# Transposed score blocks, a leaky step on GpSimd and an earlier mask in a two-layer graph attention kernel

## The chip, the core and the metric

The kernel runs as one program on one core of a Trainium2 chip. The metric is the device time of one execution in microseconds; the profile gives the span from the first to the last instruction of one execution.

## The reference, cut to what matters

There are 16 graphs of 1024 nodes with 256 features, and an adjacency matrix of 0 and 1 (drawn with a share of about 3% ones, and ones on the diagonal).

```python
# layer 0: masked attention with 8 heads of 32, residual
h = relu(layernorm(x))
Q, K, V = h @ Wq.T + bq, h @ Wk.T + bk, h @ Wv.T + bv          # per head
attn = softmax(where(adj == 0, -inf, Q @ K.T * 32 ** -0.5))
x = x + (attn @ V) @ Wo.T + bo
# layer 1: edge scores of one kind where adj == 1, residual
h = relu(layernorm(x))
e_0 = leaky_relu(einsum('bid,bjd->bij', h * a_0[:, 0], h), 0.2)  # e_1..e_3 the same with a_1..a_3
scores = where(adj == 1, e_0, -9e15)                              # then 2: e_1, 3: e_2, 4: e_3
x = x + softmax(scores) @ h
```

The product inside the leaky function is symmetric in i and j: the score of (i, j) is the sum over d of h[i, d] a[d] h[j, d]. The leaky function takes y to y where y is positive and to 0.2 y where it is not.

## The kernel before, in words

The nodes of a graph are cut into 8 tiles of 128 rows, so there are 128 tiles. The main loop has 129 steps `s`, and in each step it works on several tiles at once, at different stages: `now` is the tile whose 8 heads of layer 0 are attended to in this step, `nxt` and `nxt2` are the next two, `was` is the tile before (its output product, its residual `x1`, its norm for layer 1), `gone` the one before that (its normed rows are transposed into `h1T`), `edge` is the tile of layer 1, nine tiles behind `now`, whose scores and softmax are made, `edge_was` the one before (its product with the rows of `h1`, and its output), and `piece` a tile of a later graph whose queries, keys and values are projected.

Each step loops over `h` from 0 to 7, one head of `now` in each turn, and parts of the other tiles' work are put by hand between the heads (`if h == 2: ...`). The kernel stands under a manual schedule: every engine runs its instructions in the order in which the code issues them, and waits at the one whose inputs or buffers aren't ready. The DMA issues of SyncE and GpSimd stand in the same orders.

For each head of `now`, TensorE makes 128 x 1024 scores into one of two PSUM places (`sides[0]`, and `sides[1]` for heads 3, 5 and 7; L435), VectorE adds the mask, writes the result to one of four buffers `p` and keeps the row's extreme (`softmax_max`, L447), ScalarE takes the exponential (L455). Heads 0, 1, 4 and 5 are then transposed by VectorE in blocks (L376) and placed by DMA, the other four by TensorE (L555) with copies by ScalarE (L556). Then come the products with the values (L490).

For the edge tile, `prepare` makes `ha`, the tile's columns of `h1T` times `a_0` (GpSimd, L577, at h = 4 of the step before); `score` multiplies it with all of `h1T` into `sides[1]`, one half of 512 columns at h = 0 and one at h = 1 (L587); `softmax_max` at h = 2 adds the mask, changes the sign and keeps the row's smallest value `top` (VectorE, L601), from which a small instruction makes the leaky value `nmx` (L606); `leak` at h = 4 applies the leaky step to the 128 x 1024 values in place (VectorE, L609); `softmax_exp` at h = 6 takes the exponential (ScalarE, L613). Since the sign is changed, the leaky step is a minimum: min(0.2 y, y).

The mask of a tile: the adjacency rows are loaded into `adj` (one buffer) at h = 4, two tiles ahead. At h = 3 of the step before its use, `flag` on ScalarE writes into `neg` and sums up which kinds of edges occur (L427), and then `mask` on GpSimd writes the mask over it (L415). A tile's mask is kept until its turn as edge tile.

The norm of `was` and of the next `piece` (`norms`, at h = 5) takes sums on VectorE (L188, L189) and then a chain of small GpSimd instructions (L162 to L178). `was.normed` (ScalarE, L523) uses it at h = 7, `gone.turn_normed` (TensorE, L530) and `turned_normed` (ScalarE, L534) follow in the next step at h = 0 and 1. `reciprocals` at h = 1 makes `wide` on GpSimd (L474) from the sums of the heads, `turned_reciprocals` at h = 2 copies its transposed form `recT` (ScalarE, L484), `add_bias` at h = 2 adds `bo` to the loaded rows `xb` (GpSimd, L419), and `edge_was.load_nodes` at h = 2 issues a load on GpSimd's queue (L619).

The last graph's edge tiles 1 to 7 come after the loop, in a tail where `sides` alternate and nothing of layer 0 runs. `layer_1_of_kinds` is a second way for layer 1, taken only for graphs with other kinds of edges than 0 and 1.

Of the kernel before, what the change touches and what calls it, by code (L numbers as in the profile page):

```python
# [8 lines left out]
F32 = mybir.dt.float32  # L9
# [5 lines left out]
ALU = mybir.AluOpType  # L15
AX = mybir.AxisListType

P = 128
HEADS = 8
HD = 32  # L20
# [3 lines left out]
SLOPE = 0.2  # L24
# [18 lines left out]
def gnn_kernel(  # L43
# [18 lines left out]
    nc = tc.nc  # L62
    B, N, D = x.shape
    NT = N // P
# [319 lines left out]
        return pT.rearrange("p (a j q) -> p j a q", a=NB, j=NT)  # L384


    h1s, h1Ts, x1ds, masks = {}, {}, {}, {}
    kinds_seen = const.tile([P, B * NT], F32, name="kinds_seen")

    class Attend:  # L390
# [122 lines left out]
        def keep(self):  # L513
            if self.t == 0:
                x1ds[self.b] = dram.tile([N, D], F32, tag=f"x1d{self.b}", name=f"x1d_{self.b}", bufs=1)
            nc.sync.dma_start(out=x1ds[self.b][self.rows, :], in_=self.x1)

        def normed(self):
            if self.t == 0:
                h1s[self.b] = graph.tile([P, NT, D], F32, tag="h1", name=f"h1_{self.b}")  # L520
                h1Ts[self.b] = graph.tile([P, NC, N], F32, tag="h1T", name=f"h1T_{self.b}")
            r, shift = self.norm
            nc.scalar.activation(  # L523
                h1s[self.b][:, self.t, :], self.x1, AF.Relu, bias=shift[:, 0:1], scale=r[:, 0:1]
            )
# [6 lines left out]

        def turned_normed(self):
            nc.scalar.copy(  # L534
                h1Ts[self.b][:, :, self.rows].rearrange("p c (b k) -> p c b k", b=NB),
                self.h1_ps.rearrange("p c (k b) -> p c b k", b=NB),
            )

# [20 lines left out]
    class Edges:  # L559


        def __init__(self, b, t, last=False):
            self.b, self.t = b, t
            self.rows = slice(t * P, (t + 1) * P)
            self.side = sides[t % 2 if last else 1]
            self.tags = {"sel": ("p", 4), "pT1": ("pT", 7)} if last else {}
            if last and t % 2:
                self.tags |= {"ha": ("hT", 1), "x1b": ("x1", 1)}
# [5 lines left out]
        def prepare(self):  # L574
            self.ha = self.buffer("ha", [P, NC, P])
            for c in range(NC):
                nc.gpsimd.tensor_scalar(  # L577
                    self.ha[:, c].rearrange("p (k b) -> p k b", b=NB),
                    h1Ts[self.b][:, c, self.rows].rearrange("p (b k) -> p k b", b=NB),
                    a_t[:, c, 0:1], 0.0, ALU.mult, ALU.add,  # L580
                )

        def score(self, nh):
            cols = slice(nh * HALF, (nh + 1) * HALF)
            self.e = self.side
            for c in range(NC):
                nc.tensor.matmul(  # L587
                    self.e[:, cols],
                    lhsT=self.ha[:, c, :],
                    rhs=h1Ts[self.b][:, c, cols],  # L590
                    start=(c == 0),
                    stop=(c == NC - 1),
                )

        def softmax_max(self):
            self.sel = self.buffer("sel", [P, N])
            top = small.tile([P, 1], F32, tag="top")  # L600
            nc.vector.tensor_tensor_reduce(  # L601
                out=self.sel, in0=self.e, in1=masks[self.b, self.t], scale=-1.0, scalar=3e38,
                op0=ALU.add, op1=ALU.min, accum_out=top,
            )
            self.nmx = small.tile([P, 1], F32, tag="nmx1")
            nc.vector.scalar_tensor_tensor(self.nmx, top, SLOPE, top, ALU.mult, ALU.min)  # L606

        def leak(self):
            nc.vector.scalar_tensor_tensor(self.sel, self.sel, SLOPE, self.sel, ALU.mult, ALU.min)  # L609

        def softmax_exp(self):
            self.total = small.tile([P, 1], F32, tag="total")
# [30 lines left out]

    def layer_1_of_kinds(b):
        h1 = graph.tile([P, NT, D], F32, tag="h1", name=f"h1g_{b}")
        h1T = graph.tile([P, NC, N], F32, tag="h1T", name=f"h1Tg_{b}")
        for t in range(NT):
            rows = slice(t * P, (t + 1) * P)
            xt = work.tile([P, D], F32, tag="x1", bufs=1)
            nc.sync.dma_start(out=xt, in_=in_order(x1ds[b][rows, :]))  # L650
            mv = stats_place(1)
            stats_of(xt, mv[:, 0, :])
            r, shift = norm_of(mv)
            nc.scalar.activation(h1[:, t, :], xt, AF.Relu, bias=shift[:, 0:1], scale=r[:, 0:1])
            tr = by_chunk((early, brief)[t % 2])
            for c in range(NC):
                nc.tensor.transpose(tr[:, c, :], h1[:, t, c * P : (c + 1) * P], ident)
            nc.scalar.copy(h1T[:, :, rows], tr)
        for t in range(NT):
            rows = slice(t * P, (t + 1) * P)  # L660
            at = work.tile([P, N], I32, tag="adj", bufs=1)
            nc.sync.dma_start(out=at, in_=adj[b, rows, :])
            xt = work.tile([P, D], F32, tag="x1b", bufs=1)
            nc.sync.dma_start(out=xt, in_=in_order(x1ds[b][rows, :]))

            code = work.tile([P, N], BF16, tag="neg", bufs=KEPT)
            nc.gpsimd.tensor_scalar(code, at, 5.0, 0.0, ALU.min, ALU.max)
            sel = work.tile([P, N], F32, tag="sel", bufs=1)
            nc.vector.memset(sel, NEG_INF)
            for k in range(N_KINDS):  # L670
# [15 lines left out]
                nc.vector.copy_predicated(sel, is_k, e)  # L686
            nc.vector.scalar_tensor_tensor(sel, sel, SLOPE, sel, ALU.mult, ALU.max)
            nmx = small.tile([P, 1], F32, tag="nmx1")
            nc.vector.tensor_reduce(nmx, sel, AX.X, ALU.max, negate=True)
            total = small.tile([P, 1], F32, tag="total")  # L690
            nc.scalar.activation(sel, sel, AF.Exp, bias=nmx, scale=1.0, accum_out=total)
            pT = ptp.tile([P, NT, P], F32, tag="pT1", name="pT1g", bufs=1)
            for half in range(2):
                turn_half(sel, pT, half)
            o = late
            for j in range(NT):
                nc.tensor.matmul(o, lhsT=pT[:, j, :], rhs=h1[:, j, :], start=(j == 0), stop=(j == NT - 1))
            rec = small.tile([P, 1], F32, tag="rec1")
            nc.vector.reciprocal(rec, total)
            ot = work.tile([P, D], F32, tag="ot", bufs=1)  # L700
            nc.vector.scalar_tensor_tensor(ot, o, rec, xt, ALU.mult, ALU.add)
            nc.sync.dma_start(out=out[b, rows, :], in_=ot)
# [18 lines left out]
    with tc.manual_schedule():  # L721
# [48 lines left out]
        for s in range(B * NT + 1):  # L770
# [9 lines left out]
            for h in range(HEADS):  # L780
# [25 lines left out]
                    now.softmax_max(h)  # L806
                if h == 6 and edge_was:
                    edge_was.store()
                if h == 4 and edge:
                    edge.leak()  # L810


                if ending:
# [1 line left out]

                if h == 1 and gone:
                    gone.turned_normed()


                if h == 3:  # L820
# [27 lines left out]
                if h == 1:  # L848
# [6 lines left out]
                    if piece_was:  # L855
                        piece_was.write_again()
                if h == 2:
                    if piece_was:
                        piece_was.values()
                    if was:  # L860
                        was.turn_reciprocals()
                        was.turned_reciprocals()
                        was.add_bias()
                    if edge_was:
                        edge_was.load_nodes()
                if h == 3:
                    if nxt:
                        nxt.load_queries()
                        nxt.flag()
                        nxt.mask()  # L870
                if h == 4:
                    if was:
                        was.output()
# [44 lines left out]
        for i in range(1, len(tiles) + 2):  # L918
# [9 lines left out]
            if i >= 2:  # L928
                tiles[i - 2].load_nodes()
            if edge:  # L930
                edge.softmax_max()
                edge.leak()
                edge.softmax_exp()
# [58 lines left out]
```

## Time and profile before

| | |
|---|---|
| Time, three runs | 3210.05, 3190.67, 3208.38 us; median 3208.38 us |
| Span of the profiled execution | 3197.8 us, 97634 instructions, mean granted TensorE clock 0.985 |
| TensorE busy, matmuls (PE) | 3033.3 us, 95% |
| VectorE busy (DVE) | 2797.9 us, 87% |
| ScalarE busy (ACT) | 2454.3 us, 77% |
| GpSimd busy (POOL) | 1728.1 us, 54% |
| DMA | 762.90 MB, mean 239 GB/s |

The profiled execution's own time is its span: the profile page gives no other. A row of the timeline reads: start in us, length in us, engine, line of the kernel, operation, output and input, shapes, count, and in brackets how long the engine had been idle before it and what released it. In a group, "x120 | 146.0, 1216" means 120 instructions, 146.0 us in all, 1216 ns each. A busy share is an average over stages and engines work beside each other; what a piece of work costs depends on who waits for it.

### The profile page before, as it was taken

What the parts mean: (1) busy time and instruction counts of PE and PEld (TensorE: products, weight loads), DVE (VectorE), ACT (ScalarE), POOL (GpSimd) and SP (SyncE); (2) the same over time, 40 slices, a digit from 0 to 9 for tenths busy, and PEclk for the clock granted to TensorE, in tenths of its full rate; (3) what the DMA queues carried; (4) which work ended last, traced back from release to release, by engine and by line L of the source; (5) the groups of instructions that cost most, each with busy time, mean ns of one, the idle gap of its engine ahead of it and who ended that gap; (6) DMA issues with size and microseconds to landing.
All of it is one profiled execution on the core that took longest, in us unless ns stands there. A gap on an engine that the chain in (4) does not pass through costs nothing. (4 is left out here: it accounts for less than half of the span.)

```text
span 3197.8 us, 97634 instructions
## 1 busy us (share of the span) xinstructions
PE 3033.3 (95%) x36018; PEld 2216.3 (69%) x36018; DVE 2797.9 (87%) x5111; ACT 2454.3 (77%) x4829; POOL 1728.1 (54%) x3883
## 2 busy tenths in 40 slices
PE   5889999999999999999999999999999999998998
PEld 3667767777677777777677777777767677776663
DVE  3888989899898998989899998998989889898984
ACT  3887878788787877878788787887878778787761
POOL 2555555555555555555555655555555655555541
PEclk8999999999999999999999999999999999999999
DMA  6787788887888788788887878788887878888653
GB/s 226 219 244 233 227 273 233 259 240 231 270 240 272 226 253 249 226 277 234 252 238 230 275 233 273 230 254 263 235 272 226 269 228 232 267 240 249 194 161 91
DMA packets 747156, 762.90 MB, mean 239 GB/s; under 512 B 71281, under 2 KB 692209, under 8 KB 746673
## 3 DMA queue, kind: packets, MB, share of 16 engines
q1 hardware_dynamic: 678432, 542.34, 58.3%
q0 software_dynamic: 65040, 210.03, 20.3%
q8 instruction: 290, 4.75, 0.6%
q10 hardware_dynamic: 3200, 4.19, 0.4%
q14 instruction: 194, 1.58, 0.1%
HBM read 252.98 MB, written 167.77 MB: 132 GB/s over the span
## 5 line engine op out<-in xcount | busy, mean ns | idle before, releaser
L455 ACT ACTIVATE p<-p,nmx 128x1024 f32<-128x1024 f32 x1024 | 1178.5, 1151 | 249.6 <-DVE nmx L447 248.9
L447 DVE CUSTOM_DVE_ANT_0 p<-s,neg 128x1024 f32<-128x1024 f32 x1024 | 1233.3, 1205 | 92.0 <-issue 49.8
L435 PE MATMUL s<-k,qt 128*128 128x512 f32 x2048 | 795.0, 469 | 77.6 <-DMA qt<-qd 57.4
L415 POOL TENSOR_SCALAR neg<-adj 128x1024 bf16<-128x1024 int32 x128 | 466.8, 3647 | 411.8 <-ACT neg L427 411.8
L376 DVE STREAM_TRANSPOSE blocks<-p 128x1024 f32<-128x1024 f32 x520 | 642.3, 1235 | 11.3 <-ACT p L613 10.8
L556 ACT COPY pT<-trp 128x512 f32<-128x512 f32 x1024 | 543.6, 581 | 86.5 <-PE trp L555 78.6
L490 PE MATMUL acc<-pT,v 128*32 128x128 f32 x16384 | 525.1, 277 | 25.7 <-DMA pT<-blocks 24.3
L555 PE MATMUL trp<-ident,p 128*128 128x128 f32 x4096 | 534.7, 274 | 0.1
L555 PEld LDWEIGHTS trp<-ident,p 128*128 128x128 f32 x4096 | 480.9, 141 | 72.5 <-ACT pT L556 3.0
L490 PEld LDWEIGHTS acc<-pT,v 128*32 128x32 f32 x16384 | 450.7, 111 | 97.6 <-DVE ot L640 41.2
L631 PE MATMUL acc<-h,pT 128*32 128x256 f32 x8192 | 495.8, 383 | 4.0 <-DVE ot L640 3.2
L435 PEld LDWEIGHTS s<-k,qt 128*128 128x128 f32 x2048 | 330.3, 192 | 210.2 <-issue 122.6
L587 PE MATMUL s<-h1T,ha 128*128 128x512 f32 x992 | 471.1, 598 | 0.0
L631 PEld LDWEIGHTS acc<-h,pT 128*32 128x32 f32 x8192 | 242.6, 110 | 208.4 <-issue 58.7
L474 POOL COPY wide<-rec 128x256 f32<-128x256 f32 x128 | 50.8, 397 | 491.4 <-DVE rec L472 491.4
L321 POOL DMA_DIRECT2D kd<-halves x240 | 168.8, 703 | 228.7 <-DVE halves L294 216.2
L601 DVE CUSTOM_DVE_ANT_0 sel<-s,neg 128x1024 f32<-128x1024 f32 x120 | 147.0, 1225 | 126.4 <-PE s L587 126.4
L587 PEld LDWEIGHTS s<-h1T,ha 128*128 128x128 f32 x992 | 171.5, 193 | 124.1 <-issue 124.1
L455 ACT ACTIVATION_READ_ACCUMULATOR p<-p,nmx 128x1 f32 x1024 | 193.4, 189 | 0.0
L484 ACT COPY recT<-acc 128x256 f32<-128x256 f32 x128 | 47.8, 373 | 177.3 <-PE acc L480 177.3
L273 PEld LDWEIGHTS acc<-hT,wkT 128*128 128x128 f32 x960 | 120.8, 197 | 76.7 <-issue 47.3
L273 PE MATMUL acc<-hT,wkT 128*128 128x128 f32 x960 | 144.3, 295 | 27.3 <-DVE halves L294 26.1
(126 smaller groups left out, 4025.1 us busy)
## 6 DMA issues: line engine op xcount, KB each, us to landing
pT<-blocks SPq DMA_DIRECT2D x2560, 128.0 KB, 3.1
qt<-qd SPq DMA_DIRECT2D x128, 512.0 KB, 5.9
adj<-in_adj POOLq DMA_DIRECT2D x127, 512.0 KB, 5.5
qd<-halves SPq DMA_DIRECT2D x240, 256.0 KB, 4.6
k<-kd POOLq DMA_DIRECT2D x120, 512.0 KB, 6.8
kd<-halves POOLq DMA_DIRECT2D x240, 128.0 KB, 3.4
kd<-halves SPq DMA_DIRECT2D x240, 128.0 KB, 3.2
xb<-in_x POOLq DMA_DIRECT2D x128, 128.0 KB, 3.4
```

What stands on the lines that cost most here:

```text
L273: nc.tensor.matmul(ps, lhsT=wT[:, fc, oc * P : (oc + 1) * P], rhs=(self.hT, self.hTm)[which][:, fc, :], start=(fc == 0), stop=(fc == NC - 1),)
L321: queue.dma_start(out=kds[self.b][oc, :, :, twice, self.cols], in_=halves.rearrange("p (w n) -> p w n", w=2),)
L376: nc.vector.transpose(blocks.rearrange("p b j q -> p j b q"), p)
L415: nc.gpsimd.tensor_scalar(self.neg, self.adj, 0.0, MASKED, ALU.is_equal, ALU.mult)
L435: nc.tensor.matmul(self.ps[:, cols], lhsT=self.qt[:, h, :], rhs=keysets[self.b][h][:, cols], start=True, stop=True,)
L447: nc.vector.tensor_tensor_reduce(out=p, in0=sides[h in (3, 5, 7)], in1=self.neg, scale=-SCALE, scalar=FLOOR, op0=ALU.add, op1=ALU.min, acc ...
L455: nc.scalar.activation(p, p, AF.Exp, bias=nmx, scale=-1.0, accum_out=self.sums[:, h : h + 1])
L490: nc.tensor.matmul(sums_place[r * HD : (r + 1) * HD, g * P : (g + 1) * P], lhsT=vs[self.b][:, j, place_of(h) : place_of(h) + HD], rhs=self ...
L555: nc.tensor.transpose(tr[:, j, :], p[:, jj * P : (jj + 1) * P], ident)
L556: copy(pT[:, half * 4 : half * 4 + 4, :], tr)
L587: nc.tensor.matmul(self.e[:, cols], lhsT=self.ha[:, c, :], rhs=h1Ts[self.b][:, c, cols], start=(c == 0), stop=(c == NC - 1),)
L631: nc.tensor.matmul(sums_place[a * HD : (a + 1) * HD, :], lhsT=self.pT[:, j, a], rhs=h1s[self.b][:, j, :], start=(j == 0), stop=(j == NT - 1),)
```

## The change

There are three parts.

The scores of layer 1 are symmetric before the leaky step. With the change, an edge tile t multiplies only for the column blocks t to 7. After that, ScalarE copies the blocks right of the diagonal from PSUM into a new place `mirror` (`keep`, at h = 1 and h = 2, one instruction for each contiguous place), and later tiles get their blocks left of the diagonal by a transpose of the kept copy on TensorE. `h1T` becomes one buffer for all graphs, and `mirror` has 16 blocks of 128 x 128, which are used again as they are read.

The leaky step of the edge tiles in the main loop goes from VectorE to GpSimd, and is issued at the end of h = 3 and not at h = 4. `softmax_max` scales by -0.2, and the leaky value is y + 4 min(y, 0): on GpSimd two instructions for the row's extreme and two for each quarter of 256 columns. The last graph's tiles in the tail keep it on VectorE.

`flag` and `mask` move from h = 3 to h = 2, where they stand ahead of `values`, the reciprocals' transposes, `add_bias` and `edge_was.load_nodes`.

```diff
+    h1T = const.tile([P, NC, N], F32, name="h1T")
+    mirror = const.tile([P, NT // 2, NT // 2, P], F32, name="mirror")
+    def mirrored(t, first, end):
+        half = NT // 2
+        if t >= half:
+            return [mirror[:, first - t - 1 : end - t - 1, t - half, :]]
+        places = []
+        for j in range(first, min(end, half)):
+            row, at = (half - 1, t) if j == half - 1 else (half - 2, t + j - 1)
+            places.append(mirror[:, row, at : at + 1, :])
+        if end > half:
+            places.append(mirror[:, t, max(first, half) - half : end - half, :])
+        return places
+    def mirrored_block(t, j):
+        return mirrored(t, j, j + 1)[0][:, 0, :]
...
         def score(self, nh):
-            cols = slice(nh * HALF, (nh + 1) * HALF)
-            self.e = self.side
-            for c in range(NC):
-                nc.tensor.matmul(
-                    self.e[:, cols],
...
+            first, end = nh * NT // 2, (nh + 1) * NT // 2
+            for j in range(first, min(end, self.t)):
+                block = self.side[:, j * P : (j + 1) * P]
+                nc.tensor.transpose(
+                    block.rearrange("p (b k) -> p k b", b=NB), mirrored_block(j, self.t), ident
+                )
+            cols = slice(max(first, self.t) * P, end * P)
+            if self.t < end:
+                for c in range(NC):
+                    nc.tensor.matmul(
+                        self.side[:, cols],
+                        lhsT=self.ha[:, c, :],
+                        rhs=h1T[:, c, cols],
...
+        def keep(self, nh):
+            first, end = max(nh * NT // 2, self.t + 1), (nh + 1) * NT // 2
+            for place in mirrored(self.t, first, end) if first < end else ():
+                width = place.shape[1]
+                blocks = self.side[:, first * P : (first + width) * P]
+                nc.scalar.copy(
+                    place.rearrange("p j (k b) -> p j k b", b=NB),
+                    blocks.rearrange("p (j b k) -> p j k b", b=NB, k=HD),
+                )
+                first += width
...
-                out=self.sel, in0=self.e, in1=masks[self.b, self.t], scale=-1.0, scalar=3e38,
-                op0=ALU.add, op1=ALU.min, accum_out=top,
+                out=self.sel, in0=self.side, in1=masks[self.b, self.t], scale=-SLOPE, scalar=3e38,
+                op0=ALU.add, op1=ALU.min, accum_out=self.top,
...
-            nc.vector.scalar_tensor_tensor(self.nmx, top, SLOPE, top, ALU.mult, ALU.min)
-        def leak(self):
-            nc.vector.scalar_tensor_tensor(self.sel, self.sel, SLOPE, self.sel, ALU.mult, ALU.min)
+        def leak(self):
+            if self.last:
+                self.nmx = small.tile([P, 1], F32, tag="nmx1")
+                for to, y in ((self.nmx, self.top), (self.sel, self.sel)):
+                    nc.vector.scalar_tensor_tensor(to, y, 1 / SLOPE, y, ALU.mult, ALU.min)
+                return
+            g = nc.gpsimd
+            less = small.tile([P, 1], F32, tag="less1")
+            g.tensor_scalar(less, self.top, 0.0, 1 / SLOPE - 1, ALU.min, ALU.mult)
+            g.tensor_tensor(self.nmx, self.top, less, ALU.add)
+            part = N // 4
+            for i in range(4):
+                sel = self.sel[:, i * part : (i + 1) * part]
+                less = work.tile([P, part], F32, tag="less", bufs=1)
+                g.tensor_scalar(less, sel, 0.0, 1 / SLOPE - 1, ALU.min, ALU.mult)
+                g.tensor_tensor(sel, sel, less, ALU.add)
...
-                if h == 4 and edge:
-                    edge.leak()
...
+                if h in (1, 2) and edge:
+                    edge.keep(h - 1)
...
                 if h == 2:
+                    if nxt:
+                        nxt.flag()
+                        nxt.mask()
                     if piece_was:
                         piece_was.values()
...
                 if h == 3:
                     if nxt:
                         nxt.load_queries()
-                        nxt.flag()
-                        nxt.mask()
+                    if edge:
+                        edge.leak()
...
             if edge:
+                edge.keep(0)
+                edge.keep(1)
                 edge.softmax_max()
```

More of the change, by code (lines that the diff above doesn't have):

```diff
@@ L384, in placed @@
         return pT.rearrange("p (a j q) -> p j a q", a=NB, j=NT)
-    h1s, h1Ts, x1ds, masks = {}, {}, {}, {}
+    h1s, x1ds, masks = {}, {}, {}
+    h1T = const.tile([P, NC, N], F32, name="h1T")
[13 more added lines that the diff above has]
+        return mirrored(t, j, j + 1)[0][:, 0, :]
     kinds_seen = const.tile([P, B * NT], F32, name="kinds_seen")
@@ L520, in normed @@
                 h1s[self.b] = graph.tile([P, NT, D], F32, tag="h1", name=f"h1_{self.b}")
-                h1Ts[self.b] = graph.tile([P, NC, N], F32, tag="h1T", name=f"h1T_{self.b}")
             r, shift = self.norm
@@ L534, in turned_normed @@
             nc.scalar.copy(
-                h1Ts[self.b][:, :, self.rows].rearrange("p c (b k) -> p c b k", b=NB),
+                h1T[:, :, self.rows].rearrange("p c (b k) -> p c b k", b=NB),
                 self.h1_ps.rearrange("p c (k b) -> p c b k", b=NB),
@@ L562, in __init__ @@
         def __init__(self, b, t, last=False):
-            self.b, self.t = b, t
+            self.b, self.t, self.last = b, t, last
             self.rows = slice(t * P, (t + 1) * P)
@@ L578, in prepare @@
                     self.ha[:, c].rearrange("p (k b) -> p k b", b=NB),
-                    h1Ts[self.b][:, c, self.rows].rearrange("p (b k) -> p k b", b=NB),
+                    h1T[:, c, self.rows].rearrange("p (b k) -> p k b", b=NB),
                     a_t[:, c, 0:1], 0.0, ALU.mult, ALU.add,
@@ L583, in score @@
         def score(self, nh):
-            cols = slice(nh * HALF, (nh + 1) * HALF)
-            self.e = self.side
-            for c in range(NC):
-                nc.tensor.matmul(
-                    self.e[:, cols],
[L589 to L592, printed above, removed]
-                )
+            first, end = nh * NT // 2, (nh + 1) * NT // 2
[3 more added lines that the diff above has]
+                    block.rearrange("p (b k) -> p k b", b=NB), mirrored_block(j, self.t), ident
+                )
@@ new lines, in score @@
+            cols = slice(max(first, self.t) * P, end * P)
[5 more added lines that the diff above has]
+                        rhs=h1T[:, c, cols],
+                        start=(c == 0),
+                        stop=(c == NC - 1),
+                    )
[9 more added lines that the diff above has]
+                first += width
@@ L598, in softmax_max @@
         def softmax_max(self):
             self.sel = self.buffer("sel", [P, N])
-            top = small.tile([P, 1], F32, tag="top")
+            self.top = small.tile([P, 1], F32, tag="top")
             nc.vector.tensor_tensor_reduce(
-                out=self.sel, in0=self.e, in1=masks[self.b, self.t], scale=-1.0, scalar=3e38,
-                op0=ALU.add, op1=ALU.min, accum_out=top,
-            )
-            self.nmx = small.tile([P, 1], F32, tag="nmx1")
-            nc.vector.scalar_tensor_tensor(self.nmx, top, SLOPE, top, ALU.mult, ALU.min)
@@ L645, in layer_1_of_kinds @@
         h1 = graph.tile([P, NT, D], F32, tag="h1", name=f"h1g_{b}")
-        h1T = graph.tile([P, NC, N], F32, tag="h1T", name=f"h1Tg_{b}")
         for t in range(NT):
```

## The prediction

> **What bounds the kernel now.** I read the table by stretches first, then one ordinary step of the main loop engine by engine, then the list of waits. Four consecutive steps, cut from mask to mask:
>
> ```profile
> 1282.30:1305.50 23.20, 23.20 (x284) 17.15 (x283) 21.73 (x42) 19.22 (x39) 12.98 (x30) 1.00 0.80 227
> 1305.50:1328.69 23.19, 23.19 (x284) 17.13 (x283) 21.73 (x42) 19.24 (x39) 12.99 (x30) 1.00 0.80 240
> ```
>
> The columns are length, then busy time of PE, weight load, DVE, ACT and GpSimd (POOL). PE is busy for the whole 23.20 us at full granted clock: PE sets the ordinary step. DVE (21.73) and ACT (19.22) follow, POOL has 12.98. From the first edge tile's maximum (267.61) to that of step 127 (3084.58) lie 118 steps in 2816.97 us, so the mean step is 23.87 us: 23.2 and a few longer ones around the key loads.
>
> A busy share hides order, so the second view is POOL's own order in that step, and where ACT stands beside it:
>
> ```profile
> 1282.30 3.65 POOL L415 TENSOR_SCALAR neg<-adj 128x1024 bf16<-128x1024 int32 x1 [3.24 <-ACT neg L427]
> 1286.05 0.98 POOL L577 TENSOR_SCALAR ha<-h1T,a_t 128x128 f32<-128x128 f32 x2
> 1286.96 0.60 POOL L406 DMA_DIRECT2D adj<-in_adj  x1
> 1287.74 0.22 POOL L162 TENSOR_SCALAR ve<-mv 128x2 f32<-128x2 f32 x1 [0.18 <-DVE mv L189]
> ...
> 1292.54 0.23 POOL L178 TENSOR_SCALAR shift<-shift 128x2 f32<-128x2 f32 x1
> ...
> 1300.89 0.88 POOL L419 TENSOR_TENSOR xb<-xb,bo_t 128x256 f32<-128x256 f32 x1
> 1301.56 0.70 POOL L619 DMA_DIRECT2D x1b<-x1d  x1
> 1305.50 3.64 POOL L415 TENSOR_SCALAR neg<-adj 128x1024 bf16<-128x1024 int32 x1 [3.24 <-ACT neg L427]
> ```
>
> ```profile
> 1289.99 1.13 ACT L613 ACTIVATE sel<-sel,nmx 128x1024 f32<-128x1024 f32 x1
> ...
> 1292.81 0.60 ACT L523 ACTIVATE h<-x,shift,r 128x256 f32<-128x256 f32 x1
> ...
> 1304.17 1.13 ACT L427 ACTIVATE neg<-adj,less_half 128x1024 bf16<-128x1024 int32 x1
> ```
>
> This is a loop through two in-order queues. ACT's check of kinds (L427) releases POOL's mask (L415); behind it stand the two ha products, the adjacency load and the norm's chain, which ends at 1292.77; ACT's normed tile (L523) starts 0.04 us later; ACT then works through its exponentials to the next L427. The loop's POOL half is 10.5 us, its ACT half 12.7 us. It closes in one step only because ACT has idle places in it:
>
> ```profile
> POOL neg L415 <- ACT neg L427: 411.8, 128, 27.8
> ACT recT L484 <- PE acc L480: 177.3, 128, 1.5
> ACT h L523 <- POOL shift L178: 32.8, 32, 5.0
> ```
>
> (us in total, times, longest.) ACT waits for PE and DVE, and already 32 times for POOL's norm. POOL's 46% of idle time is therefore not all free: most lies in the half where it waits for ACT.
>
> **The change, part by part.** All prices are against the profiled execution, span 3197.8 us. The three runs of before gave 3190.67 to 3210.05, median 3208.38, so span and median differ by 0.3% and I add nothing between them. About 1% is what a measurement of this kernel can tell from no change.
>
> *PE, score blocks.* Before, two halves of 4 matmuls took 1.88 us each, 0.47 us per block of 128 columns. Now tile t transposes t blocks and multiplies 8 - t. Transposes in the trace go 8 in 1.03 us, 0.13 us each. With 3.5 blocks per tile on average: 3.5 x (0.47 - 0.13) = 1.2 us less PE per step.
>
> *DVE.* The leaky step (L609, 1.22 us) and its small one (L606, 0.37 us) go: 1.6 us of 21.7.
>
> *ACT, copies kept.* 13 copies per 8 tiles. From L556 (512 columns, 581 ns) and L534 (256 columns, 371 ns) the price is 0.16 us plus 0.82 ns per column: 0.58, 0.48, 0.37 and 0.27 us for 4, 3, 2 and 1 blocks. The second call averages 0.43 us per step, the first 0.20: 0.63 us. Their slots are on ACT's half of the loop. They also guard sides[1], which scores(3) overwrites; but the tile's maximum (DVE, ends at 1301.4) does that later than the copy would (about 1300.6), so that guard is hidden.
>
> *Check and mask one step earlier.* On ACT the check moves ahead of recT (0.37 us) and of one exponential (1.15 us). On POOL the mask now stands ahead of xb+bo and the x1b load, which were done in its waiting time before: they come behind it and cost 0.68 + 0.58 us by their spacing. xb+bo is needed by the residual on DVE, some 6 us later even in a step of 23.2 us, the x1b load by the store later still, at h = 6: hidden.
>
> *POOL, the leaky step.* Ten instructions: two on one column, 0.23 and 0.20 us; four pairs on 256 columns; each waits for the one before, and waiting neighbours in the norm's chain stand 0.08 us apart. The second of a pair is a two-input add of the shape of L419: 0.86 us (0.72 at its quickest in the last steps). The first, minimum and multiply with one f32 input, is not in the trace. Bounds: the copy L474 of 256 columns, 0.40 us; the mask, (3.65 - 0.22) / 1022 = 3.35 ns per column, hence 1.07 us. Nearest is ha (L577), f32 to f32 with two operations: 0.50 us for 128 columns against 0.22 for 2, 2.25 ns per column, hence 0.79 us. I take 0.79. Sum: 0.59 + 4 x (0.79 + 0.86 + 0.16) = 7.8 us, from 5.7 (0.40 and 0.72) to 9.0 us.
>
> The Trainium skill (GPSIMD Engine Reference, sections 3.1 and 4.1) prices one-input work near line rate, about 1.03 cycles a column at 1.2 GHz, and two-input adds at 2.6 cycles, and advises the vector engine for elementwise work. Of the rows the copy agrees (0.83 ns per column), ha and the mask do not (2.25 and 3.35). By the page the leaky step would be an estimated 6.0 us and the total some 3515 us; slower too.
>
> *The loop, closed again.* Behind the leaky step stand, on POOL, ha (0.91 us by spacing), the adjacency load (0.68) and the norm's chain (5.03); ACT's edge exponential waits for the leaky step, ACT's normed tile for the norm, and behind these wait the exponentials and so PE's transposes. POOL's half: 3.72 mask + 1.26 + 7.84 + 0.91 + 0.68 + 5.03 = 19.4 us, plus 5 key loads of 0.6 us per 8 steps, 0.4. ACT's half, back to back: 0.07 latency, 0.60 normed, three exponentials at 1.15, two pairs of copies at 1.06, 0.37 h1T, 0.63 kept copies, 1.23 check, 0.08 latency = 8.55 us. Together 28.4 us. The same sum without the leaky step is 20.5 us, below PE's 23.2: the leaky step alone turns the slack into the bound. PE's and DVE's savings then buy nothing, since both wait.
>
> Against the mean step: 28.4 - 23.87 = 4.5 us. 119 steps hold an edge tile and a full set of heads: +535 us. In the tail the leaky step stays on DVE and PE sets the pace (7.2 us per tile); at most 28 transposes x 0.34 = 9 us are saved there, while the loop's last step, short of other work, loses about 5. I book -3. 3197.8 + 535 - 3 = 3730 us.
>
> **The rivals.**
>
> *Hidden on POOL (the other side).* POOL's busy share says 11 us are free in each step; then PE's 1.2 us count: 3197.8 - 119 x 1.2 = 3055 us. It decides if the whole leaky step takes less than 23.87 - 20.5 = 3.4 us, that is 0.7 us for a pair with its gaps. Against it: the add alone took 0.72 us at its quickest, and ACT waits for POOL already.
>
> *Cheap first operation.* At the copy's rate and the quickest add, the leaky step is 5.7 us, the loop 26.2 us: 3197.8 + 119 x 2.3 = 3475 us. For it: one f32 input. Against: ha, the same form, is slower than the copy.
>
> *Dear first operation.* At the mask's rate the loop is 29.5 us, and PE may enter it:
>
> ```profile
> 3118.86 6.19 PE L587 MATMUL s<-h1T,ha 128*128 128x512 f32 x8
> 3124.88 3.60 PE L587 MATMUL s<-h1T,hT 128*128 128x512 f32 x8
> ```
>
> After PE had idled 3.3 us the same eight matmuls took 6.19 us, then 3.60. Two waits of nearly 4 us in each step could slow PE's transposes in ACT's half by some 0.5 us. 119 x 6.1 more: about 3925 us.
>
> TensorE: Matmul & The Clock Gate in the Trainium skill (part 1) puts half rate after an idle window of about 3.4 us, in line with these two rows. By it PE would run slow after each stall, an estimate of under 2 us per step, which PE, with 6 us free, can mostly pay.
>
> **How the numbers follow.** Forecast 0.65, cheap first operation 0.16, dear 0.15, hidden 0.04. The predicted time is the forecast's, 3730 us. The range runs between the two prices of the unknown operation, 3470 to 3930 us. Faster by over 1% comes only from the hidden case, 0.03; within 1%, 0.01 for a part of it eaten by the copies; slower, 0.96.
>
> **What the changed profile would show.** Right: steps of 28 us; ACT's edge exponential waiting some 3.6 us a step for POOL's last leaky add (POOL gets there 12.9 us after the check, ACT after 9.3), ACT's normed tile 3.8 us a step for POOL's norm, both over 400 us in total; the wait of the mask for the check still there; PE's busy time down by about 145 us and its share near 78%; POOL near 70%. The pairs near 1.65 us. Wrong: PE above 90% busy with POOL's waits unchanged (hidden case), or a wait that ends last elsewhere, on DVE or on the copies kept.

## The result, and the profile after

| | before | after |
|---|---|---|
| Time, median of 4 runs | 3209.22 us | 3945.12 us (3940.7 to 3954.88) |
| Ratio after to before | | 1.231, 95% interval 1.227 to 1.235 |
| Span of the profiled execution | 3197.8 us | 3941.6 us |
| PE / DVE / ACT / POOL busy | 95 / 87 / 77 / 54% | 82 / 67 / 63 / 67% |
| Mean granted TensorE clock | 0.985 | 0.915 |

The change costs 23%. It was forecast at 3730 us with a range to 3930. The direction and the loop that was named held; the size was 215 us short, and the time lies just above the range.

First the table by stretches, two steps cut from mask to mask, with the same columns as before (length, PE, weight load, DVE, ACT, POOL, granted clock, DMA share, GB/s):

```profile
1601.27:1631.11 29.84, 25.23 (x286) 18.71 (x285) 20.55 (x39) 19.29 (x40) 20.69 (x39) 0.89 0.62 182
1631.11:1659.27 28.16, 23.67 (x287) 18.14 (x286) 20.46 (x39) 19.20 (x40) 20.69 (x40) 0.94 0.67 193
```

No engine is busy for the whole step any more; the one with the most is still PE. Steps are near 30 us, and the granted clock has fallen. POOL's order in the first of these steps (start, length, engine, line, operation):

```profile
1601.27 3.64 POOL L435 TENSOR_SCALAR neg<-adj 128x1024 bf16<-128x1024 int32 x1 [4.66 <-ACT neg L447]
1604.99 0.73 POOL L439 TENSOR_TENSOR xb<-xb,bo_t 128x256 f32<-128x256 f32 x1
1605.67 0.60 POOL L670 DMA_DIRECT2D x1b<-x1d  x1
...
1606.93 1.09 POOL L659 TENSOR_SCALAR less<-sel 128x256 f32<-128x256 f32 x1
1608.10 0.74 POOL L660 TENSOR_TENSOR sel<-sel,less 128x256 f32<-128x256 f32 x1
...
1616.34 0.22 POOL L162 TENSOR_SCALAR ve<-mv 128x2 f32<-128x2 f32 x1
...
1621.13 0.23 POOL L178 TENSOR_SCALAR shift<-shift 128x2 f32<-128x2 f32 x1
...
1631.11 3.65 POOL L435 TENSOR_SCALAR neg<-adj 128x1024 bf16<-128x1024 int32 x1 [4.05 <-ACT neg L447]
```

From the mask to the end of the norm POOL works without a pause, 1601.27 to 1621.36: 20.1 us, where before it was 10.5. The leaky step is the part from 1606.35 to 1614.73, 8.4 us. ACT beside it:

```profile
1614.78 1.16 ACT L664 ACTIVATE sel<-sel,nmx 128x1024 f32<-128x1024 f32 x1 [2.82 <-POOL sel L660]
...
1621.40 0.60 ACT L542 ACTIVATE h<-x,shift,r 128x256 f32<-128x256 f32 x1 [3.73 <-POOL shift L178]
...
1629.51 0.37 ACT L630 COPY mirror<-s 128x256 f32<-128x256 f32 x1 [1.92 <-DVE top L639]
1629.78 1.15 ACT L447 ACTIVATE neg<-adj,less_half 128x1024 bf16<-128x1024 int32 x1
```

The bracket is ACT's idle time just before, and what ended it. The first two are the waits that were forecast. The third was not: the kept copy waits for VectorE's maximum, and the check of kinds (L447), which releases the next mask, stands behind it. The list of waits over the whole run (us in total, times, longest) says the same:

```profile
POOL neg L435 <- ACT neg L447: 506.4, 127, 27.9
ACT h L542 <- POOL shift L178: 474.3, 120, 5.2
...
ACT sel L664 <- POOL sel L660: 359.7, 119, 9.2
...
ACT mirror L630 <- DVE top L639: 176.7, 105, 3.1
```

I cut the main loop at the end of the norm (L178) and at the start of the mask, and took means over 118 steps:

| us per step | POOL's half | ACT's half | step |
|---|---|---|---|
| before | 10.76 | 13.16 | 23.9 |
| forecast for after | 19.8 | 8.55 | 28.4 |
| after | 20.34 | 9.85 | 30.2 |

By this cut the two halves fill the step. The excess over the forecast is 0.5 + 1.3 = 1.8 us, times 118 steps some 215 us: all that is missing. The experiments had to show what the 1.3 us are, and whether the leaky step alone carries the loss.

### The profile page after: what moved, and what is told of

Read it like the earlier page. It is cut to its first block, busy times and chain, and to the rows that moved or that the text cites. A ratio compares the mean times of both kernels' runs of the same rounds, so it can differ in the third digit from the quotient of the medians.

```text
span 3941.6 us, 98929 instructions
## 1 busy us (share of the span) xinstructions
PE 3233.7 (82%) x36210; PEld 2361.6 (60%) x36210; DVE 2648.5 (67%) x4871; ACT 2497.5 (63%) x5037; POOL 2650.0 (67%) x5083
## 5 line engine op out<-in xcount | busy, mean ns | idle before, releaser
L455 PE MATMUL s<-k,qt 128*128 128x512 f32 x2048 | 841.3, 494 | 138.7 <-DMA k<-kd 69.8
L574 PE MATMUL trp<-ident,p 128*128 128x128 f32 x4096 | 630.3, 304 | 158.3 <-ACT p L475 119.0
L574 PEld LDWEIGHTS trp<-ident,p 128*128 128x128 f32 x4096 | 535.4, 157 | 308.5 <-ACT p L475 164.2
L659 POOL TENSOR_SCALAR less<-sel 128x256 f32<-128x256 f32 x480 | 514.1, 1071 | 40.1
L639 DVE CUSTOM_DVE_ANT_0 sel<-s,neg 128x1024 f32<-128x1024 f32 x120 | 146.9, 1225 | 349.8 <-PE s L616 282.9
L660 POOL TENSOR_TENSOR sel<-sel,less 128x256 f32<-128x256 f32 x480 | 351.3, 732 | 40.0
L542 ACT ACTIVATE h<-x,shift,r 128x256 f32<-128x256 f32 x128 | 76.8, 600 | 474.3 <-POOL shift L178 474.3
L664 ACT ACTIVATE sel<-sel,nmx 128x1024 f32<-128x1024 f32 x120 | 138.1, 1151 | 359.7 <-POOL sel L660 359.7
L616 PE MATMUL s<-h1T,ha 128*128 128x512 f32 (+2 forms) x744 | 353.4, 608 | 10.2 <-ACT mirror L630 9.1
L549 PE MATMUL acc<-ident,h 128*128 128x128 f32 x256 | 66.4, 349 | 331.9 <-ACT h L542 331.9
L294 DVE SCALAR_TENSOR_TENSOR halves<-acc,bk_t,halves 128x128 fp32r<-128x128 f32 x240 | 83.3, 347 | 350.7 <-PE acc L549 244.6
```

Source lines behind the costliest of these rows:

```text
L455: nc.tensor.matmul(self.ps[:, cols], lhsT=self.qt[:, h, :], rhs=keysets[self.b][h][:, cols], start=True, stop=True,)
L574: nc.tensor.transpose(tr[:, j, :], p[:, jj * P : (jj + 1) * P], ident)
L616: nc.tensor.matmul(self.side[:, cols], lhsT=self.ha[:, c, :], rhs=h1T[:, c, cols], start=(c == 0), stop=(c == NC - 1),)
L659: g.tensor_scalar(less, sel, 0.0, 1 / SLOPE - 1, ALU.min, ALU.mult)
L660: g.tensor_tensor(sel, sel, less, ALU.add)
```

## The experiments

A second table serves several of them: the mean length of a step by the number of the edge tile in its graph, from the starts of the edge maximum (L601 before, L639 after). Tiles 6 and 7 are the steps with the key loads.

| step of tile | 0 | 1 | 2 | 3 | 4 | 5 | 6 | 7 | mean |
|---|---|---|---|---|---|---|---|---|---|
| before | 23.24 | 23.19 | 23.28 | 23.22 | 23.28 | 23.35 | 25.55 | 26.14 | 23.87 |
| 1: leaky step on DVE | 24.15 | 23.94 | 23.38 | 23.33 | 22.79 | 22.53 | 26.83 | 27.75 | 24.29 |
| 5: transposed blocks alone | 24.08 | 23.85 | 23.10 | 23.20 | 22.72 | 22.28 | 25.95 | 26.47 | 23.92 |
| 6: early mask alone | 23.40 | 23.61 | 23.48 | 23.45 | 23.56 | 23.32 | 28.59 | 27.43 | 24.54 |
| 8: as 5, without copies | 22.79 | 22.63 | 22.57 | 22.48 | 22.31 | 21.96 | 26.23 | 25.38 | 23.25 |
| 9: as 5, projection first | 23.49 | 23.16 | 22.59 | 22.69 | 22.49 | 22.08 | 25.86 | 26.49 | 23.56 |

**1. The leaky step back on VectorE, the rest of the change kept.**

```diff
-            if self.last:
+            if True:
...
-            g = nc.gpsimd
...
+                if h == 4 and edge:
+                    edge.leak()
```

> The changed kernel with the leaky step of the main loop back on VectorE at h = 4 (one instruction on the row's extreme, one on 128 x 1024); transposed blocks, kept copies and the earlier mask stay. Theory A (the leaky step in GpSimd's queue is the whole loss; the loop through ACT and POOL falls from 30.0 us to below 22 us, so that PE with 1.2 us less work sets the step): about 3060 to 3110 us, ACT's waits for POOL's last add gone and for POOL's norm back to some tens of us, granted clock back at 0.98. Theory B (the kept copies and their waits on ACT, and the transposes, cost as much by themselves): above 3250 us, with ACT's copy to mirror waiting for VectorE's maximum as now.

Measured: 3250.24 us, ratio to before 1.0154 (1.0116 to 1.0191). Neither theory came out whole: the time stands at theory B's bound, yet of the 736 us lost 695 go with the leaky step, and the step is 24.3 us, not 30.2. But the kernel is not faster than before, as theory A wanted: PE's 1.2 us are not there. Two places show it. Around the edge maximum of a tile 0, on three engines:

```profile
1245.05 1.22 DVE L639 CUSTOM_DVE_ANT_0 sel<-s,neg 128x1024 f32<-128x1024 f32 x1 [1.43 <-ACT p L475]
...
1246.31 0.59 ACT L630 COPY mirror<-s 128x512 f32<-128x512 f32 x1 [1.34 <-DVE top L639]
...
1246.95 0.72 PE L455 MATMUL s<-k,qt 128*128 128x512 f32 x2 [0.48 <-ACT mirror L630]
```

The maximum reads `sides[1]`, the copy, which the kernel issues after it, reads the same place once it is done, and the scores of head 3, which overwrite it, come after the copy. Before, they had only the maximum to wait for. The Trainium skill (PSUM — Partial Sum Buffer, section on bank collisions) says that two engines may not touch one PSUM bank in the same partitions at once, two reads included, so that software puts them in order; the trace agrees as far as it goes: the copy waits for the maximum 91 times in this kernel, 91.9 us in all. The second place is the wait of PE for keys, before and in this run:

```profile
PE s L435 <- DMA k<-kd: 4.4, 5, 1.7
```

```profile
PE s L455 <- DMA k<-kd: 36.1, 22, 3.2
```

**2. The kept copy behind the check of kinds.**

```diff
-                if h in (1, 2) and edge:
-                    edge.keep(h - 1)
+                if h == 1 and edge:
+                    edge.keep(0)
...
                     if nxt:
                         nxt.flag()
                         nxt.mask()
+                    if edge:
+                        edge.keep(1)
```

> The changed kernel with the second kept copy issued behind the check of kinds and the mask at h = 2, no longer ahead of them. Theory A (the step is 30.0 us because two in-order halves add up, and ACT's half grew from the 8.55 us of the prediction to some 9.8 us since the kept copy, which stands ahead of the check, waits for VectorE's maximum of the edge tile): the copy (0.43 us) and its wait (1.5 us) leave the loop, 119 x 1.9 us, so about 3715 us, the same wait standing behind the check. Theory B (ACT's half is set by PE's slow clock after its stall, and the copy's wait is only where it shows): within 40 us of 3941. Theory C (scores of head 3 now wait for the later copy and PE passes that on): above 3941.

Measured: 3887.0 us (3879.25 to 3894.74). A miss for A: 58 us came back, not 230. ACT's half fell by 0.43 us to 9.42, which is the length of the copy and no more. The wait had not gone, it had moved to the check itself:

```profile
ACT neg L447 <- DVE top L639: 189.4, 118, 3.1
```

The check writes a mask buffer. There are ten (`KEPT = LAG + 1`), and the mask of the next tile takes the one that the edge tile, nine tiles behind, reads in its maximum in this very step. At h = 3 the maximum was over; at h = 2 it is issued just ahead. So the check waits for VectorE with or without the copy. Theory B's number is missed too (54 us below 3941, not within 40). The wait of theory C did grow, from 60.5 us in the changed kernel to

```profile
PEld s L455 <- ACT mirror L630: 177.9, 105, 2.7
```

but the time did not rise above 3941. This result could not yet tell a wait that decides from one that only covers PE's lateness.

**3. One operation in the first instruction of a pair.**

```diff
-                g.tensor_scalar(less, sel, 0.0, 1 / SLOPE - 1, ALU.min, ALU.mult)
+                g.tensor_scalar(less, sel, 0.0, None, ALU.min)
```

> The changed kernel with the first instruction of each pair on GpSimd reduced to one operation, the minimum; the product with 4 is left out, so the leaky slope is another. Theory A (two operations are why a quarter of 256 columns takes 1.07 us and not the 0.40 us of a copy): 0.4 to 0.7 us each, 1.5 to 2.7 us less per step, and since the loop passes it on in full, 3620 to 3760 us. Theory B (a tensor-scalar instruction costs 3.3 to 4 ns per column whatever it does): 1.07 us as before, time within 15 us of 3941.

Measured: 3812.96 us, one run. The group (busy us, mean ns):

```profile
L659 POOL TENSOR_SCALAR less<-sel 128x256 f32<-128x256 f32 x480 | 408.1, 850 | 31.9
```

It is 0.85 us with one operation against 1.07 with two, between the theories: the second operation costs 0.22 us, and most of the price is there with one. POOL's half fell by 0.96 us and the step by 1.07. In this one run the loop passes the saving on in full, as the forecast's closing needed.

**4. The leaky step on GpSimd alone.**

```diff
                     if nxt:
                         nxt.load_queries()
                         nxt.flag()
                         nxt.mask()
+                    if edge:
+                        edge.leak()
...
-                if h == 4 and edge:
-                    edge.leak()
```

> The kernel before with the leaky step on GpSimd alone, issued at the end of h = 3 behind the mask; full score matmuls, no kept copies, check and mask at h = 3. Theory A (the leaky step in the queue is the whole loss): POOL's half 3.7 mask + 8.4 leaky step + 0.6 for the extreme included + 6.6 for ha, load and norm + 0.4 = 19.1 us, ACT's half 9.4 us, 28.5 us a step: 3198 + 119 x 4.6 = 3750 us, with the two waits of ACT for POOL as in the changed kernel. Theory B (the early check and the kept copies carry a good part of the loss): below 3550 us.

Measured: 3950.1 us, ratio 1.2334 (1.2274 to 1.2394): this part alone costs as much as the whole change. Theory B is out. That the two times are nearly equal is a coincidence of two differences, which the halves below show. The two waits of ACT for POOL stand first among ACT's:

```profile
ACT sel L626 <- POOL sel L622: 498.2, 119, 9.1
ACT h L523 <- POOL shift L178: 476.8, 122, 5.2
```

But A's 3750 us are missed by 200. POOL's half is 18.87 us, as worked out (19.1), 1.5 us less than in the whole change, mostly since `add_bias` and the load of `x1b` don't stand behind the mask. ACT's half is 11.36 us, not 9.4, and 1.5 us more than in the whole change. The 9.4 us were ACT's own work back to back. With the check at h = 3, the copy of the reciprocals (`recT`) stands ahead of the check and waits for PE, as it did before:

```profile
ACT recT L484 <- PE acc L480: 158.4, 121, 3.4
```

In this half that is 1.3 us a step, and waits for VectorE's maxima are another 0.6: together the 2 us. With the check at h = 2 the wait for `recT` is out of the loop (2.6 us in all in the changed kernel), and the wait for the edge maximum is in it. How much of the 2 us goes back to PE's late restart was not tried.

**5. The transposed blocks and kept copies alone** (leaky step on VectorE at h = 4, check and mask at h = 3).

> The kernel before with the transposed blocks and kept copies alone: leaky step on VectorE at h = 4, check and mask at h = 3. The first experiment, which had the early mask as well, took 3250 us; its steps with key loads were 1.3 and 1.6 us longer than before's (26.83 and 27.75 against 25.55 and 26.14). Theory A (the early mask costs there, because it stands ahead of the key loads of h = 3 and h = 4 in GpSimd's queue): those two come back to 25.6 and 26.2 us, 15 x 2.9 = 43 us less, about 3207 us, PE's wait for key loads back from 36 us to some 5 us. Theory B (the copies and transposes cause it): 3240 to 3255 us.

Measured: 3195.47 us over 10 runs, ratio 0.9975 (0.9946 to 1.0004). Theory A: against experiment 1 the steps of tiles 6 and 7 get 0.9 and 1.3 us shorter, and PE's wait for keys falls from 36.1 to 6.1 us. The transposed blocks alone can't be told from no change. The table shows why: against before, the steps of tiles 4 and 5 are 0.6 and 1.1 us shorter, and those of tiles 0 and 1, with three and two copies of single blocks at h = 1 and nothing or little to transpose, 0.8 and 0.7 us longer.

**6. The early mask alone.**

```diff
                 if h == 2:
+                    if nxt:
+                        nxt.flag()
+                        nxt.mask()
                     if piece_was:
                         piece_was.values()
...
                 if h == 3:
                     if nxt:
                         nxt.load_queries()
-                        nxt.flag()
-                        nxt.mask()
```

> The kernel before with check and mask at h = 2 and not at h = 3, nothing else. Theory A (the same 43 us from the key loads behind the mask): about 3240 us, with PE waiting some 35 us more for key loads. Theory B (the early mask is free, ACT having idle time there): within 15 us of 3201.

Measured: 3278.69 us, ratio 1.0225 (1.0152 to 1.0298). Theory B is out; A has the direction and the wait, but not the size, 72 us and not 40. PE's wait for keys rose from 4.4 to 39.8 us, and the check waits for the maximum here too:

```profile
ACT neg L427 <- DVE top L601: 142.0, 118, 1.2
...
PE s L435 <- DMA k<-kd: 39.8, 15, 3.7
```

By the table it costs 5.6 us over eight steps, 4.3 of them in the two with key loads. GpSimd's queue there shows a key load behind the mask (with `add_bias` and the `x1b` load between them) that the kernel before issues ahead of it:

```profile
808.31 3.65 POOL L415 TENSOR_SCALAR neg<-adj 128x1024 bf16<-128x1024 int32 x1 [1.76 <-ACT neg L427]
...
813.32 0.56 POOL L356 DMA_DIRECT2D k<-kd  x1
```

PE's longer wait is about half of the 72 us; what makes up the other half was not separated.

**7. The late copy, and an eleventh mask buffer.**

```diff
-    KEPT = LAG + 1
+    KEPT = LAG + 2
...
-            self.recT = work.tile([P, NC, P], F32, tag="recT", bufs=1)
+            self.recT = work.tile([P, NC, P], F32, tag="wide", bufs=1)
...
-                less = work.tile([P, part], F32, tag="less", bufs=1)
+                less = work.tile([P, part], F32, tag="ot", bufs=1)
```

> The second experiment (late kept copy, 3887 us) with an eleventh mask buffer; for room, recT shares the place of wide and the leaky step's scratch that of the output tile. In the second experiment the check of kinds still waited 189 us for VectorE's maximum of the edge tile: with ten buffers the new mask takes the buffer that this maximum reads in the same step. Theory A (this wait is what held ACT's half of the loop at 9.4 us, and the loop passes it on): ACT's half about 7.9 us, step about 28.2 us, about 3700 us. Theory B (PE's late and slow work after its stall sets ACT's half, and the wait only covers it): above 3820 us.

Measured: 3704.84 us (3700.83 to 3708.86); ACT's half 7.78 us, step 28.16. Theory A, nearly to the number. The check no longer waits for VectorE's maximum, and ACT's half is its own work back to back: 7.78 us, where the forecast had 8.1 without the second copy. So the wait cost 1.6 us a step (9.42 - 7.78). The two shared places are a further difference of this kernel; what they bring is a new wait of VectorE for the last leaky add (67.8 us in all), which does not explain a gain. What remains in the loop:

```profile
ACT h L542 <- POOL shift L178: 462.5, 120, 5.2
...
POOL neg L435 <- ACT neg L447: 284.7, 124, 28.5
...
ACT sel L664 <- POOL sel L660: 156.8, 100, 9.1
```

The run shows that the wait for the maximum decides. It does not show that PE's clock has no part in it, for the maximum itself waits for PE's edge scores, before and in the changed kernel:

```profile
DVE sel L601 <- PE s L587: 126.4, 120, 3.0
```

```profile
DVE sel L639 <- PE s L616: 282.9, 90, 5.1
```

In the changed kernel's step shown above, these scores come after a stall of PE, at about half of the full clock (in the two stretches at the end the granted clock stands third from the right, 0.50 and 0.52):

```profile
1617.21 1.09 PE L574 MATMUL trp<-ident,p 128*128 128x128 f32 x8 [1.08 <-ACT p L475]
...
1622.05 0.69 PE L549 MATMUL acc<-ident,h 128*128 128x128 f32 x2 [3.31 <-ACT h L542]
...
1623.65 1.97 PE L574 MATMUL trp<-ident,p 128*128 128x128 f32 x8
...
1625.63 2.58 PE L616 MATMUL s<-h1T,ha 128*128 128x384 f32 x4
...
1628.24 1.23 DVE L639 CUSTOM_DVE_ANT_0 sel<-s,neg 128x1024 f32<-128x1024 f32 x1 [3.06 <-PE s L616]
```

```profile
1621.40:1624.80 3.40, 2.69 (x10) 1.97 (x11) 1.52 (x4) 3.40 (x6) 1.26 (x2) 0.50 0.84 249
1624.80:1628.00 3.20, 3.20 (x10) 2.18 (x8) 0.35 (x4) 2.79 (x7) 1.66 (x3) 0.52 0.73 223
```

The transposes take 0.9 us more than ahead of the stall, and the four products 1.2 us more than three quarters of the 1.88 us that four with 512 columns took before. By this estimate the clock delays the maximum by some 2 us, about as long as the kept copy waits for it here (1.92 us). In experiment 7 the maximum still waits 281.2 us for PE, but ACT's check doesn't wait for the maximum any more. A run with PE kept at full clock was not made, so how much of the wait is the clock's stays open.

**8. As 5, without the copies.**

```diff
-            for place in mirrored(self.t, first, end) if first < end else ():
+            for place in ():
```

> The fifth experiment without the kept copies: the place mirror is filled with zeros once, and the blocks left of the diagonal are transposed from it, so those scores are left out. Theory A (the copies take back what the transposes save, because scores of head 3 wait for the copy of sides[1], which itself starts only when VectorE's maximum is done: 0.5 to 0.7 us of PE per step, and some for the first copies): 3110 to 3140 us. Theory B (VectorE, busy 21.7 of 23.2 us, sets the step once PE is relieved): within 25 us of the fifth experiment.

Measured: 3124.9 us, ratio 0.9753 (0.9674 to 0.9832). Theory A: the copies take back 71 us of what the transposes give. This kernel leaves out the scores left of the diagonal. Even without the copies the step falls by 0.62 us, not by the 1.2 us of PE's work; what takes the rest was not followed up.

**9. As 5, the projection ahead of the scores of head 3.**

```diff
+                if h == 3 and piece_was:
+                    piece_was.project(1, 0)
+                    piece_was.project(1, 1)
                 if now:
                     now.scores(h)
...
                 if h == 3:
-                    if piece_was:
-                        piece_was.project(1, 0)
-                        piece_was.project(1, 1)
```

> The fifth experiment (transposed blocks and kept copies alone, 3195 us) with the projection of the queries at h = 3 issued on TensorE ahead of the scores of head 3, no longer behind them. Theory A (PE stands 0.5 to 0.7 us a step for the kept copy of sides[1], which starts only after VectorE's maximum; 1.05 us of projection covers it): PE's wait of 36 to 100 us for ACT's copy gone, 40 to 70 us less, 3130 to 3155 us. Theory B (VectorE is as near to the bound, its maximum of head 3 comes later by the projection, and PE's gain is lost): within 15 us of 3195.

Measured: 3153.84 us, ratio to before 0.9832 (0.9806 to 0.9858): 1.7% below the kernel before, and 42 us below experiment 5. Theory A. The copy still waits for the maximum as it did (91.2 us); PE's waits for the copy, in experiment 5 and here (PEld is the weight load ahead of the matmul):

```profile
PEld s L455 <- ACT mirror L630: 64.4, 105, 1.6
PE s L455 <- ACT mirror L630: 37.7, 89, 1.4
```

```profile
PEld s L455 <- ACT mirror L630: 10.0, 7, 1.6
```

**10. As 9, one quarter of the leaky step on GpSimd.**

```diff
+            part = N if self.last else 3 * N // 4
...
+        def leak_rest(self):
+            g = nc.gpsimd
+            sel = self.sel[:, 3 * N // 4 :]
...
+                    if edge:
+                        edge.leak_rest()
```

> The ninth kernel, and one quarter of the leaky step (256 columns, one pair) on GpSimd behind the mask at h = 3, the other three quarters and the row's extreme on VectorE at h = 4. It asks where the loop through ACT and GpSimd begins to decide. The prediction put that at 3.4 us of leaky step; the pair takes 1.07 + 0.73 + 0.16 = 2.0 us. Theory A (below the threshold it is hidden, POOL's half 12.9 us and ACT's about 10 us closing in 22.9 us; VectorE saves 0.3 us): within 25 us of the ninth kernel, either way. Theory B (each microsecond on GpSimd's queue is paid from the first one): 118 x 2.0 us more, some 235 us above the ninth kernel.

Measured: 3191.14 us, 37 us above experiment 9, outside A's 25, where the full price would have been 235. Between the theories, near A: most of the 2 us is hidden, not all. ACT's wait for the norm, in experiment 9 and here:

```profile
ACT h L542 <- POOL shift L178: 24.9, 26, 5.9
```

```profile
ACT h L542 <- POOL shift L178: 182.6, 112, 6.2
```

POOL's half is 12.77 us and ACT's 11.10; against experiment 9 the steps of tiles 0, 1 and 7 are longer by 0.4, 0.5 and 2.7 us, and that of tile 6 is 1.2 us shorter. What makes tile 7 so long was not followed up.

## Where the prediction was right, and the step of it that failed

*The loop closed by two queues* was right. The leaky step by itself costs as much as the whole change (experiment 4), taking it out gives back 695 of 736 us (1), a microsecond less on POOL is a microsecond less in the step (3, one run), and a quarter of it is mostly hidden (10), as the threshold of 3.4 us asked.

*The step that failed* is in ACT's half: "Check and mask one step earlier", with the sentence on the kept copies that their guard is hidden. I moved the check on ACT and counted what it passes (`recT`, one exponential), and put at nothing what the check itself waits for at its new place: the mask buffer that the edge maximum is just reading, and, by the copy ahead of it, the maximum itself. The copy could not end ahead of the maximum, as the sentence on the guard had it, since it starts only behind it. The forecast took 8.55 us back to back, and 9.85 were measured. Of these, 1.5 us a step are the copy's wait for the maximum (176.7 us over 118 steps). Without the waits ACT's half is 7.78 us and the time 3705 us (7).

*POOL's half* was summed to 19.8 us and measured 20.34. The term that was mis-sized is the first instruction of a pair: 0.79 us were taken from the ha product, and it is 1.07, the mask's price per column, the upper bound. The add was 0.73, near its quickest row, not 0.86. Together the leaky step took 8.4 us and not 7.8. So the excess over the forecast is about 1.3 us a step from ACT's half and 0.5 from POOL's.

*The rival "dear first operation"* named the right price of the operation, and 3925 us. For its second half it took PE's slow clock after a stall, some 0.5 us in PE's transposes. The clock did fall (0.915; the transposes of L574 took 304 ns on average against 274 before), but in this half ACT waits only some 0.15 us a step for these transposes. What ACT waits for is VectorE's maximum, and how far PE's clock stands behind that is open (7). That the rival's sum comes so near is in part luck.

*The signs.* ACT's wait for the norm was over 400 us, as forecast (474.3); its wait for the last leaky add was not (359.7). PE's busy time was to fall by some 145 us and rose by 200 (3033.3 to 3233.7 us): there is less work, but at a lower granted clock the same work took longer.

*"Hidden on POOL"* was priced at 3055 us, PE's saving in full. The runs speak against that saving too, though it wasn't the forecast: with the leaky step on VectorE the rest of the change takes 3250 us (1). The early mask costs 72 us alone (6). On GpSimd's queue it stands ahead of key loads, which the prediction counted as 0.4 us of queue and did not follow to PE, and PE's wait for them is about half of the 72 us. The copies take back most of the transposes' saving (5, 8) until PE has other work in that place (9).

## What to carry to other kernels

Idle time on an engine is not spare time until the loop through its queue has been closed: add the work behind the new instructions to the work of the engine that waits for them, and compare with the step. When an instruction is moved earlier, ask first what it waits for at the new place, the reader of its buffer above all, and then what it now stands ahead of in its queue. A copy that reads a place which another engine also reads may hold back whoever overwrites it; other work put ahead of that writer can cover it.

## What the runs showed of the hardware that I had not expected

GpSimd's minimum and multiply on 256 f32 columns takes 1.07 us, and with the minimum alone 0.85 us, while its two-input add on the same shape takes 0.73: the one-input form was the dearer one. The Trainium skill (GPSIMD Engine Reference, section 4.1) puts one-input work roughly at line rate. At the 1.03 cycles an element and 1.2 GHz of that page, and with the 0.22 us of a row on two columns, that makes an estimate of 0.44 us. The copy's 0.40 us agrees with the page; for the minimum, with or without the multiply, the measurement decides against it. For a two-input add the page's section 3.1 has about 2.6 cycles an element; with the 0.20 us of such an add on two columns that makes an estimate of 0.75 us, and the 0.73 us agree.
